# Reordering filler matmuls and gate projections in a graph recurrence

## The chip, the core and the metric

The kernel runs on one core of a Trainium2 chip. The metric is device time in microseconds (us) of one execution; the table below gives three timed runs and one profiled execution. The core's engines work side by side, each on its own instructions in their written order: TensorE (PE in the profile; PEld are its weight loads), VectorE (DVE), ScalarE (ACT), GpSimd (POOL) and SyncE (SP, which only issues DMAs here). They wait for each other through semaphores. "Matmul" below means one call of the program on float32 data with 256 columns; the trace shows each as two passes of the array ("x24" is 12 calls), and two passes start 0.22 us apart at full clock, so that one call is 0.447 us.

## The reference, cut to what matters

Sixteen graphs of 1024 nodes with 256 features go through four residual layers. Layers 0, 1 and 3 are dense products with the adjacency matrix and are not touched. Layer 2 is a recurrence over the nodes:

```python
norm_adjT = jnp.swapaxes(adj, 1, 2) * dinv[:, :, None]
def step(h, i):
    x = jnp.take(h_e, i, axis=1)
    row = jnp.take(norm_adjT, i, axis=1)
    x_par = jnp.einsum('bj,bjd->bd', row, h)
    iou = x @ W_ioux.T + b_ioux + x_par @ W_iouh.T + b_iouh
    r, z = jnp.split(iou, 2, axis=1)
    r, z = (jax.nn.sigmoid(r), jax.nn.sigmoid(z))
    hc = jnp.tanh(x @ W_coux.T + b_coux + x_par * r @ W_couh.T + b_couh)
    h_new = z * x_par + (1.0 - z) * hc
    return jax.lax.dynamic_update_slice(h, h_new[:, None, :], (0, i, 0)), None
h_out, _ = jax.lax.scan(step, h_e, jnp.arange(n))
```

Node i sees the new values of nodes before it and the old values of those after it.

## The kernel before, in words

Layer 2 handles the nodes in 8 blocks of 128 (t = 0 to 7), each in 8 sub-blocks of 16 (s = 0 to 7). In the 128 nodes of a block an earlier step of the kernel has put mutually independent nodes next to each other, so that the 16 nodes x 16 graphs of a sub-block can mostly be computed at once. A sub-block consists of

- `x`, the weighted sum over the parents (L967 on VectorE): a base part held in `bxt` (SBUF) plus `near`, the contribution of the sub-block just finished, made by four matmuls (L1037; at the end of a block `next_block`, L771);
- a round (`round_`): matmuls into `pr` and `pz`, sigmoids (L843, L848), r times x (L844), matmuls into `pc`, tanh, the new values `hT`; then `turned`, which transposes them into `h` (L870, L873);
- a run-time branch (L1014) for a further round, `one_more`, where chains of dependent nodes ask for it;
- the scatter of `h` to HBM into `hs_d` (L1030, two indirect DMAs issued by GpSimd).

What does not depend on the chain serves as filler for TensorE: the lists `share`, `behind` and the gates' tasks.

`Gates` (L734) makes the input half of the three gates of the *next* sub-block: GpSimd copies the nodes' features into `hs` (L740), and `gate(q)` does four matmuls (L749) into one PSUM buffer `pf` (there are three of them, shared by all filler) and gives back `out`, the copy with bias to SBUF. q = 0 is r, q = 1 is z, q = 2 the candidate. For z and the candidate `out` is one VectorE instruction (L754), for r it is two ScalarE instructions (L757). Afterwards `seed_r` and `seed_zc` (L761, L764, L765) put them into the PSUM accumulators. Outs are collected in `late` and issued at the next `evict()`.

For s = 0 the gates of sub-block 1 are made inside the round, as part of `todo`. For s = 1 to 7 they are made in the arms of the branch: within `one_more`, or, where it isn't needed, in the Else arm, all three one after the other with their outs one behind. Instructions after the branch that read something which `one_more` may rewrite, such as `h`, wait for a count of the writing engine's semaphore. In the built program the Else arm makes up for `one_more`'s instructions by a larger step (21) on the first instruction of an engine in that arm, and the last one brings the count to the arm's end. `near` (L1037) waits for ScalarE's count at the arm's end (974 in one of the places), for VectorE's 3351, which the first VectorE out of the arm passes, and for TensorE's own last gate matmul; L771 and the scatter L1030 wait for ScalarE's alone.

`base_tasks(t + 1)` (L597) makes `bxt` of the next block: for each of the 16 graphs a task of seven matmuls (L637), one for each block of 128 parents except block t, from adjacency `ab` and features `hb`. The features come from three places: `hn_d` for blocks long finished, `hs_d[t - 1]` for the block finished last (L609), and `he_d` for those still old. So the matmul over parent block t - 1, the one with index k = t - 1 of the seven, needs the DMA L609, which reads what the scatter at the end of block t - 1 has written. A mask (L615, GpSimd) is laid over one tile of `ab`. `last_tasks` (L666) adds the last missing part of `bxt` from `hr`, 512 KB loads out of `hs_d` (L675). SyncE issues in this order after a block's last scatter: three `hr` loads, L609 for graph 0, L609 for graph 1, a copy to `hn_d` (L943).

For s = 0, `todo` is the three gates (cost 1.72 each), the seven base matmuls of graph 0 (0.43 each, `share`) and up to 16 `last_tasks` (0.4 each, `behind`). `fill(weight)` takes tasks from its front: a first portion before `x` is computed, a second one (weight 1.3) inside the round after the `pc` matmuls, the rest in `turned`. `todo` is a fixed list, and for the four compute engines layer 2 keeps the written order; only SyncE's order is chosen by the framework's scheduler.

Where layer 2 ends, the first additions of layer 3 (L1113, VectorE) stand early in block 7 and need `hs_d[6]` too.

Of the kernel before, what the change touches and what calls it, by code (L numbers as in the profile page):

```python
# [40 lines left out]
def gnn_stack(ctx: ExitStack, tc: tile.TileContext, a: dict, out: bass.AP):  # L41
# [520 lines left out]
    def layer_2(shared, early):  # L562
        with ExitStack() as st:
# [102 lines left out]
            def last_tasks(t, bxt):  # L666

                n = P - S
                loaded = {}

                def load(b0):
                    ao = big.tile([P, 4, n], F32, name="ao", bufs=3)
                    nc.sync.dma_start(ao, next_d[b0 : b0 + 4, t - 1].rearrange("b p i -> p b i"))
                    hr = big.tile([P, 4, D], F32, name="hr", bufs=3)
                    nc.sync.dma_start(hr, hs_d[t - 1][b0 // GB][b0 % GB * P : (b0 % GB + 4) * P]  # L675
                                      .rearrange("(b p) d -> p b d", p=P))
                    loaded[b0] = ao, hr

                def task(b):
                    def run():  # L680
                        b0 = b - b % 4
                        ao, hr = loaded[b0]
                        if b % 4 == 0 and b + 12 < B:
                            load(b + 12)
                        pl = psum.tile([P, DC, n], F32, name="pf", bufs=3)
                        for c in range(DC):
                            nc.tensor.matmul(pl[:, c], hr[:, b - b0, c * P : (c + 1) * P], ao[:, b - b0],
                                             start=True, stop=True)
                        to = bxt[:, :, b, S:]
                        return lambda: nc.vector.tensor_add(to, to, pl)  # L690
                    return 0.4, run
                for b0 in (0, 4, 8):
                    load(b0)
                return [task(b) for b in range(B)]

            def load_he(t):
                he = big.tile([P, DC, B, P], F32, name="he")
                for c in range(DC):
                    nc.sync.dma_start(he[:, c], heT_d[:, :, c, t * P : (t + 1) * P].rearrange("b p i -> p b i"))
                return he  # L700
# [4 lines left out]
            class Sub:  # L705
# [3 lines left out]
                def __init__(self, t, s):  # L709
                    self.s = s  # L710
                    self.n = P - s * S + (S if t + 1 < NT else 0)
                    self.aj = big.tile([P, G2, P + S], F32, name="aj")
                    for g in range(G2):
                        nc.gpsimd.indirect_dma_start(out=self.aj[:, g], out_offset=None, in_=near_d[:, :],
                                                     in_offset=row(0, g, t, s))
# [18 lines left out]
            class Gates:  # L734


                def __init__(self, he, s):
                    self.hs = big.tile([P, DC, G2 * GR], F32, name="hs")
                    for c in range(DC):
                        nc.gpsimd.tensor_copy(self.hs[:, c].rearrange("p (b i) -> p b i", b=B),  # L740
                                              he[:, c, :, s * S : (s + 1) * S])
                    self.g = big.tile([P, 3, DC, G2 * GR], F32, name="gates")
                    self.tasks = [lambda q=q: self.gate(q) for q in (1, 2, 0)]

                def gate(self, q):
                    pg = psum.tile([P, DC, G2 * GR], F32, name="pf", bufs=3)
# [28 lines left out]
            def far_tasks(bxt, h, sub):  # L775


                bd, s = sub.bd, sub.s
                far = P - (s + 2) * S

                def task(g, c, b4):
                    def run():
                        pf = psum.tile([P, 4, far], F32, name="pf", bufs=3)
                        nc.tensor.matmul(pf, h[:, g, c * P : (c + 1) * P], bd[:, g, b4 : b4 + 4, S : S + far],  # L784
                                         start=True, stop=True)
                        to = bxt[:, c, g * GB + b4 : g * GB + b4 + 4, P - far :]
                        return lambda: nc.vector.tensor_add(to, to, pf)  # L787
                    return 0.0067 * far, run
                tasks = []
                if far > 0:  # L790
                    tasks = [task(g, c, b4) for g in range(G2) for c in range(DC) for b4 in (0, 4)]
                if sub.n > P - s * S:
                    tasks.append((0.9, lambda: next_block(h, bd, P - (s + 1) * S, s == 0)))
                return tasks
# [103 lines left out]
            with tc.manual_schedule(engines={mybir.EngineType.PE, mybir.EngineType.DVE, mybir.EngineType.Activation, mybir.EngineType.Pool}):  # L898
# [17 lines left out]
                behind = []  # L916
                for t in range(NT):
# [10 lines left out]
                    for s in range(NS):  # L928
# [4 lines left out]
                        share = [task for _ in range(BASES[s] if base_todo else 0) for task in base_todo.popleft()]  # L933
                        todo, gx_next = [], None
                        if s == 0:
                            gx_next = Gates(he, 1)
                            todo = [(1.72, task) for task in gx_next.tasks] + share + behind
                        else:
                            if s == 1 and t + 1 < NT:
                                he_next = load_he(t + 1)  # L940
                            if s == 1 and t > 0:
                                for g in range(G2):
                                    nc.sync.dma_start(hn_d[g * GB : (g + 1) * GB, (t - 1) * P : t * P],  # L943
                                                      hs_d[t - 1][g].rearrange("(b p) d -> b p d", p=P))
                            lists = [behind, share]
                            sizes = [len(x) for x in lists]
                            while any(lists):
                                i = max(range(2), key=lambda i: len(lists[i]) / max(sizes[i], 1))
                                todo.append(lists[i].pop(0))
# [83 lines left out]
                        if s + 1 < NS:  # L1033
# [5 lines left out]
                            behind = far_tasks(bxt, h, sub)  # L1039
                        elif t + 1 < NT:  # L1040
                            next_block(h, sub.bd, 0, False)
                            near = pnx
                            behind = last_tasks(t + 1, bxt_next)
# [172 lines left out]
    with tc.tile_pool(name="shared", bufs=2) as shared:  # L1216
        x, hn, at = {}, {}, {}
        layer_2(shared, lambda: early_3(shared, x, hn, at))
        layer_3(shared, x, hn, at)
# [46 lines left out]
```

## Time and profile before

| what | us |
|---|---|
| three timed runs | 4899.82, 4900.79, 4907.13 (median 4900.79) |
| profiled execution | 4910.16 |
| its span, first to last instruction | 4908.1 |
| layer 2, from 1507 to 3450 in the span | 1943.0, TensorE busy 1748.29 of it |
| mean granted TensorE clock | 0.975 |

How to read the profile's lines. In the timeline a line gives start, duration, engine, source line, operation, what is written<-read, shape and number of instructions merged, and in brackets the idle time of that engine before it with what ended the idle time. SPq is SyncE issuing DMAs. In the list of waits a line gives who waited for whom, the total in us, how often and the longest. The windows view gives, for a stretch of time, each engine's busy time, the granted TensorE clock (1.00 is full), the DMA engines' share and GB/s.

### The profile page before, as it was taken

What the parts mean: (1) busy time and instruction counts of PE and PEld (TensorE: products, weight loads), DVE (VectorE), ACT (ScalarE), POOL (GpSimd) and SP (SyncE); (2) the same over time, 40 slices, a digit from 0 to 9 for tenths busy, and PEclk for the clock granted to TensorE, in tenths of its full rate; (3) what the DMA queues carried; (4) which work ended last, traced back from release to release, by engine and by line L of the source; (5) the groups of instructions that cost most, each with busy time, mean ns of one, the idle gap of its engine ahead of it and who ended that gap; (6) DMA issues with size and microseconds to landing.
All of it is one profiled execution on the core that took longest, in us unless ns stands there. A gap on an engine that the chain in (4) does not pass through costs nothing. (4 is left out here: it accounts for less than half of the span.)

```text
span 4908.1 us, 52731 instructions
## 1 busy us (share of the span) xinstructions
PE 4510.6 (92%) x18307; PEld 3022.5 (62%) x18307; DVE 2290.3 (47%) x6408; ACT 1213.9 (25%) x2651; POOL 1586.5 (32%) x1947
## 2 busy tenths in 40 slices
PE   8898899999987999899999999988799999999999
PEld 4443455555555777777777777777465555555656
DVE  6667754465553444444444444344524334344342
ACT  1211112122211222222322222222223223223232
POOL 3122233443333322232222323232524334234231
PEclk9999999999998999999999999999899999999999
DMA  5333326545536444444444444430422222232200
GB/s 159 116 91 102 93 81 205 182 165 182 173 121 186 126 150 126 151 126 148 125 139 123 142 145 141 124 110 32 167 69 86 77 93 71 77 103 72 74 26 17
DMA packets 530980, 576.65 MB, mean 117 GB/s; under 512 B 42544, under 2 KB 439472, under 8 KB 528304
## 3 DMA queue, kind: packets, MB, share of 16 engines
q1 hardware_dynamic: 499536, 460.27, 30.3%
q0 software_dynamic: 31040, 111.44, 6.4%
q8 instruction: 199, 3.26, 0.3%
q14 instruction: 205, 1.68, 0.1%
HBM read 469.65 MB, written 116.65 MB: 119 GB/s over the span
## 5 line engine op out<-in xcount | busy, mean ns | idle before, releaser
L309 PE MATMUL pa<-at,h 128*128 128x512 f32 x1088 | 493.8, 606 | 32.8 <-DVE ag L314 32.8
L1141 PE MATMUL ph<-ag,w 128*128 128x512 f32 x1024 | 478.3, 610 | 32.6 <-DVE hh L1145 32.6
L637 PE MATMUL pf<-hb,ab 128*128 128x256 f32 x1568 | 435.1, 390 | 22.1 <-ACT bs L624 18.8
L1179 PE MATMUL po<-w,hh 128*128 128x256 f32 x2048 | 447.7, 379 | 0.0
L1179 PEld LDWEIGHTS po<-w,hh 128*128 128x128 f32 x2048 | 387.8, 190 | 59.3 <-issue 7.9
L309 PE MATMUL pa<-at,q 128*128 128x512 f32 x960 | 424.3, 595 | 0.0
L749 PE MATMUL pf<-hs,wx 128*128 128x256 f32 x1536 | 358.3, 390 | 30.0 <-POOL hs L740 30.0
L309 PEld LDWEIGHTS pa<-at,h 128*128 128x128 f32 x1088 | 209.0, 195 | 276.5 <-issue 230.7
L1141 PEld LDWEIGHTS ph<-ag,w 128*128 128x128 f32 x1024 | 178.5, 190 | 294.3 <-DVE hh L1145 151.7
L749 PEld LDWEIGHTS pf<-hs,wx 128*128 128x128 f32 x1536 | 297.5, 196 | 74.8 <-POOL hs L740 33.1
L1147 POOL TENSOR_TENSOR ss<-ss,sq 128x512 f32<-128x512 f32 x224 | 305.3, 1363 | 117.8 <-ACT sq L1144 113.4
L637 PEld LDWEIGHTS pf<-hb,ab 128*128 128x128 f32 x1568 | 280.8, 195 | 69.8 <-ACT bs L624 26.1
L309 PEld LDWEIGHTS pa<-at,q 128*128 128x128 f32 x960 | 178.2, 190 | 215.8 <-issue 212.8
L1030 POOL DMA_INDIRECT hs_d<-h,table x128 | 129.4, 1011 | 490.6 <-ACT gates L757 386.9
L1145 DVE TENSOR_SCALAR hh<-ph,b 128x512 f32<-128x512 f32 x256 | 190.1, 747 | 153.6 <-ACT sq L1144 120.1
L784 PE MATMUL pf<-bd,h 128*128 128x384 f32 (+5 forms) x768 | 221.9, 376 | 26.8 <-DVE bxt L787 26.8
L1126 PE MATMUL pa<-bxt,h 128*128 128x512 f32 x512 | 228.7, 599 | 18.6 <-POOL bxt L1108 18.6
L1126 PE MATMUL pa<-at,h 128*128 128x512 f32 x512 | 228.8, 597 | 0.0
L1144 ACT ACTIVATE sq<-ph,b 128x512 f32<-128x512 f32 x224 | 153.8, 687 | 233.1 <-PE ph L1141 187.9
L1171 ACT ACTIVATE hh<-hh,rw 128x512 f32<-128x512 f32 x256 | 168.9, 714 | 138.4 <-DVE hh L1170 136.6
L754 DVE TENSOR_TENSOR gates<-pf,bias 128x512 f32<-128x512 f32 x128 | 88.4, 691 | 231.6 <-PE pf L749 231.6
L1182 DVE TENSOR_TENSOR x<-x,po 128x256 f32<-128x256 f32 x120 | 50.5, 421 | 288.9 <-PE po L1179 288.9
(253 smaller groups left out, 7411.4 us busy)
## 6 DMA issues: line engine op xcount, KB each, us to landing
at<-in_adjT SPq DMA_DIRECT2D x64, 1024.0 KB
ab<-in_adj SPq DMA_DIRECT2D x128, 512.0 KB
bxt<-in_adjT SPq DMA_DIRECT2D x64, 512.0 KB
at<-in_adjT SPq DMA_DIRECT2D x64, 512.0 KB
ad<-in_adj SPq DMA_DIRECT2D x128, 128.0 KB
x_d<-x POOLq DMA_DIRECT2D x16, 1024.0 KB, 4.8
he_d<-h POOLq DMA_DIRECT2D x16, 1024.0 KB, 9.1
heT_d<-hT POOLq DMA_DIRECT2D x16, 1024.0 KB
```

The source lines that it names most:

```text
L309: nc.tensor.matmul(pa, h[:, mt, c * P : (c + 1) * P], at[n0 // 512][:, mt], start=mt == 0, stop=mt == NT - 1)
L637: nc.tensor.matmul(pb, ab[:, jts[k]], hb[:, jts[k]], start=k == 0, stop=k == len(jts) - 1)
L749: nc.tensor.matmul(pg[:, e], wx[:, c, q * D + e * P : q * D + (e + 1) * P], self.hs[:, c], start=c == 0, stop=c == DC - 1)
L784: nc.tensor.matmul(pf, h[:, g, c * P : (c + 1) * P], bd[:, g, b4 : b4 + 4, S : S + far], start=True, stop=True)
L1030: nc.gpsimd.indirect_dma_start(out=hs_d[t][g][:, :], out_offset=row(1, g, t, s), in_=h[:, g], in_offset=None)
L1126: nc.tensor.matmul(pa, h[b][:, mt, c * P : (c + 1) * P], at[b][n0 // NH][:, mt], start=mt == 0, stop=mt == NT - 1)
L1141: nc.tensor.matmul(ph, w1[:, c, k * P : (k + 1) * P], ag[:, c, n0 : n0 + NH], start=c == 0, stop=c == DC - 1)
L1144: nc.scalar.activation(sq, ph, AF.Square, bias=b1[:, k : k + 1])
L1145: nc.vector.tensor_scalar(hh[:, k], ph, b1[:, k : k + 1], None, op0=ALU.add)
L1147: nc.gpsimd.tensor_tensor(ss, ss, sq, ALU.add)
L1171: nc.scalar.activation(hh[:, k], hh[:, k], AF.Silu, scale=rw[:, k : k + 1])
L1179: nc.tensor.matmul(po, hh[:, c, k * P : (k + 1) * P], w2[:, c], start=c == 0, stop=c == HC - 1)
```

## The change

It has two parts. The gates' tasks are made in the order r, z, candidate instead of z, candidate, r, everywhere. And at s = 0 the first six of the seven base matmuls of graph 0 stand ahead of the gates in `todo`; the seventh stays behind them.

```diff
-                    self.tasks = [lambda q=q: self.gate(q) for q in (1, 2, 0)]
+                    self.tasks = [lambda q=q: self.gate(q) for q in range(3)]
...
                         if s == 0:
                             gx_next = Gates(he, 1)
-                            todo = [(1.72, task) for task in gx_next.tasks] + share + behind
+                            todo = share[:6] + [(1.72, task) for task in gx_next.tasks] + share[6:] + behind
```

In the built program this gives at the start of blocks 1 to 6 on TensorE, from `near` (L771) to the round's `pr` matmuls: before, 12 gate matmuls; after, 6 base matmuls and the 8 gate matmuls of r and z. Behind the `pc` matmuls there follow, before, 7 base matmuls; after, the 4 of the candidate and 1 base matmul; then `last_tasks` as before. The base matmul with k = t - 1 carries the wait for L609 in both. In block 0, where `behind` is empty, 8 gate matmuls stood ahead of the round, 4 gate and 4 base matmuls behind `pc`, 3 base matmuls behind the transposes; now 6 base matmuls stand ahead, the 8 of r and z behind `pc`, the candidate's 4 and the seventh base matmul behind the transposes, and the first base matmul waits for two loads and the mask. In block 7 there is no base work: `share` is empty. On GpSimd the two masks at s = 0 come ahead of the two `aj` DMA issues (L714) instead of behind them. In the Else arms ScalarE's two L757 instructions follow the first gate instead of the last, and VectorE's two L754 follow the second and third. SyncE's order is the same.

## The prediction

> **What bounds the kernel now.** I read the page first, then the list of waits on TensorE, then the timeline around a block's start, then the windows view for the clock.
>
> ```profile
> span 4908.1 us, 52731 instructions
> PE 4510.6 (92%) x18307; PEld 3022.5 (62%) x18307; DVE 2290.3 (47%) x6408; ACT 1213.9 (25%) x2651; POOL 1586.5 (32%) x1947
> ```
>
> TensorE is the bound, but in layer 2 it is idle for 1943.0 - 1748.29 = 195 us, and all it does there hangs on one chain. What counts is which wait ends last at a place, so here are three of its waits:
>
> ```profile
> PE pa L1037 <- ACT gates L757: 41.6, 42, 1.0
> ...
> PE pf L749 <- POOL hs L740: 30.0, 10, 10.9
> ...
> PE pnx L771 <- ACT gates L757: 5.2, 7, 0.9
> ```
>
> 42 times `near` waits 0.99 us for ScalarE's copy of gate r, the last thing in the Else arm; seven more times at a block's end (0.62 to 0.91). The start of block 2:
>
> ```profile
> 1996.38 0.69 DVE L754 TENSOR_TENSOR gates<-pf,bias 128x512 f32<-128x512 f32 x1 [1.40 <-PE pf L749]
> ...
> 1999.83 0.84 ACT L757 ACTIVATE gates<-pf,bias 128x256 f32<-128x256 f32 x2 [5.18 <-PE pf L749]
> ...
> 2000.35 1.16 PE L771 MATMUL pnx<-bd,h 128*128 128x128 f32 x8 [0.62 <-ACT gates L757]
> ...
> 2000.94 1.04 POOL L1030 DMA_INDIRECT hs_d<-h,table  x1 [15.12 <-ACT gates L757]
> ...
> 2003.43 1.73 SPq L675 DMA_DIRECT2D hr<-hs_d  x3
> ...
> 2003.74 7.13 PE L749 MATMUL pf<-hs,wx 128*128 128x256 f32 x24 [2.23 <-POOL hs L740]
> ...
> 2005.21 0.98 SPq L609 DMA_DIRECT2D hb<-hs_d  x2
> ...
> 2010.71 1.89 PE L802 MATMUL pr<-x,wh 128*128 128x256 f32 x8
> ...
> 2015.89 3.19 PE L637 MATMUL pf<-hb,ab 128*128 128x256 f32 x14
> ```
>
> The scatter starts when ScalarE's copies end; GpSimd copies `hs` after both scatters, so TensorE stands 2.23 us; the base matmuls come 15.5 us after `near`. L609 lies behind 1.5 MB of `hr`; by the trace's DMA completions it lands at 2011.70, 10.8 us after the scatter started (blocks 1 to 6: 11.7, 10.8, 11.0, 11.5, 10.7, 11.6). Today it is 4 us early. Block 7 shows the same chain as a wait, 11.2 us:
>
> ```profile
> 3243.02 1.04 POOL L1030 DMA_INDIRECT hs_d<-h,table  x1 [15.41 <-ACT gates L757]
> ...
> 3254.20 0.96 DVE L1113 TENSOR_TENSOR hb<-hb 128x768 f32<-128x768 f32 x1 [9.23 <-DMA hb<-hs_d]
> ```
>
> The clock is decided in stretches of 3.41 us (columns: stretch, length, PE, PEld, DVE, ACT, POOL busy, clock, DMA share, GB/s):
>
> ```profile
> 2001.42:2004.84 3.42, 1.19 (x6) 0.99 (x6) 1.36 (x3) 0.60 (x1) 2.95 (x5) 1.00 0.33 80
> 2004.84:2008.25 3.41, 3.41 (x10) 2.70 (x9) 0.69 (x1) 0.00 (x0) 1.87 (x4) 0.50 0.92 305
> 2008.25:2011.66 3.41, 3.41 (x17) 3.00 (x17) 0.69 (x1) 0.75 (x2) 0.00 (x0) 1.00 1.24 427
> ...
> 3380.41:3383.82 3.41, 3.32 (x14) 3.20 (x15) 0.91 (x4) 0.28 (x1) 1.00 (x3) 0.50 0.02 5
> 3383.82:3387.23 3.41, 3.41 (x18) 3.41 (x17) 1.24 (x5) 1.03 (x4) 0.00 (x0) 0.50 0.00 0
> ```
>
> A stretch with 2.2 us idle is followed by one at half clock (1.7 us lost); a half-clock stretch that is itself not quite full (0.09 idle) is followed by another.
>
> **The change, part by part.**
>
> *Gate r first, sub-blocks 1 to 6.* The matmuls are the same. ScalarE's copies follow the first gate, two gates (3.5 us: 1996.38 against 1999.83) earlier, so `near` no longer waits for them. Does the wait pass to VectorE, whose last copy (0.69, like ScalarE's 0.84 begun 0.1 after the last gate) is now last? If so the gain is 0.15 each, 6 us in all; if nothing is left it is 41.6. `near` needs VectorE's count only up to the arm's first copy, which ends while the last gate runs, and TensorE's own last matmul, for which I leave 0.1: **-37** (42 x 0.89). The candidate's copy, 0.69, lies beside `near` (1.16), before `x` needs VectorE; `seed_r` comes earlier on ScalarE. Where `one_more` runs, r's copies stand before the sigmoids but end within the `pr` matmuls: nothing. The earlier scatters have no reader before the block's end.
>
> *Start of blocks 1 to 6.* `near` gains its 0.62 to 0.91 and the wait for `hs` goes: with the scatter 3.45 us earlier `hs` is there in time even without the moved matmuls. But the base matmul k = t - 1, second of six in block 2, now comes 1.5 us after `near` starts, where the wait for L609 has no cover. Landing, block 2: 2011.70 - 3.45 = 2008.25, if the path runs as fast. It won't quite: the scatter then shares the DMA engines with graph 1's base load, which runs until about 2000. Scatters alone land 2.3 to 2.4 after their start, scatters beside such a load 5.5 to 6.6 (2787.69, 3028.61), each some 2.4 after the load's end; by that rule the blocks lose 0, 2.3, 1.5, 2.0, 1.4, 1.4 (bounds 0 and 4). So it lands at 2010.5; TensorE does one base matmul, stands from 2001.2 to 2010.6, then 5 base (2.2) and 8 gate matmuls (3.6), plus the clock. The stall covers whole stretches, so work resumes within a half-clock stretch, and by the rows above the next is half too: 1.7 to 3.4 lost, taken 2.56. `pr` then starts at 2019.0 instead of 2010.71: +8.3. The same sum gives +7.4, +8.3, +7.0, +7.9, +7.5, +6.4: **+44.6**. Given back: two matmuls fewer behind `pc`, 12 x 0.447 = **-5.4**; that stretch is TensorE's own (14 passes of L637, then L687 without a gap). Added: the second `last_tasks` call needs the buffer of the candidate, whose copy stands behind VectorE's `hT` work, about 0.35 each: **+2.1** (0 to 4).
>
> The Trainium skill, "TensorE: Matmul & The Clock Gate", Part 1, states a free-running window of 3413 ns, half clock after at least one idle window, full clock again after one busy window; its section on oscillation warns of just this, a DMA wait longer than a window that starts every tile cold. The rows differ twice: 2.2 us idle suffice, and a nearly full half-clock window doesn't restore the clock. By the page's rule each stall would cost 1.7 at most and the forecast would be an estimated 5 us lower. The measurement decides.
>
> *Block 0.* TensorE is free at 1521.3; gates started at 1522.55, `pr` at 1526.10. Now the first base matmul needs graph 0's features, landed at 1524.64, and the mask, which GpSimd has ready at about 1523.3. From 1524.75 six matmuls (2.7) run at half clock, since the stretch to 1523.56 is mostly idle: `pr` at 1530.1, +4.0; behind the transposes five matmuls instead of three, +0.8: **+4.8**. The `aj` issues, 3.7 us later behind the masks, are needed only when `h` is done: nothing.
>
> *Block 7* has no base work: L1113 lands 3.7 us earlier and holds VectorE less, which delayed `pc` by 3.76; one L754 fewer stands ahead of r's product: **-4.0** (-3 to -5).
>
> *Other moves.* Masks (0.55) before `aj` at blocks 1 to 6 find their load landed: nothing. The sub-blocks shift against the clock's stretches; 16 stretches in layer 2 lie at or over 1.7 us idle, some by such phase: 0, bounds -5 and +5.
>
> Sum: -37 + 44.6 - 5.4 + 2.1 + 4.8 - 4.0 = **+5 us**. Against the profiled execution that is 4910.16 to 4915; the median of the runs is 9.4 below it, and I carry the difference over: 4901 + 5 = **4906**. No change that a measurement can tell means within 0.2%, 9.8 us.
>
> **The rivals.**
>
> *A. The stall is longer, slower.* Place: L609's landing at blocks 1 to 6. Each further microsecond costs 6 us; from 0.8 us a block on it is slower by over 0.2%. For it: the scatter beside a load (up to 4 us more), `hr` loads beside it, two full half-clock stretches. At +2 us a block: 4918.
>
> *B. The stall is shorter, faster.* The graph-1 load ends before the scatter's packets flow, and the clock loses one stretch: -8.6 and -5, with the phases' -5: 4887 at the far end, 4892 in the middle. Against it: the DMA flow of 329 GB/s seen between 1998 and 1999.
>
> *C. The wait passes to VectorE.* `near` still stands 0.85 us, 42 times: +31, 4937. For it: VectorE's copy is the arm's last instruction. Against it: the count it waits for.
>
> *D. The second part does what it seems for*, fills the wait for `hs` with no stall: -37 - 4 - 6 x 2.9 - 5, 4838. That needs L609's data 9 us earlier; nothing speaks for it.
>
> **How the numbers follow.** My forecast 0.42 (within 0.2%), A 0.30, C 0.08, B 0.16, D 0.04. Faster 0.20, same 0.42, slower 0.38. The forecast's own range is 4892 to 4910; for 8 in 10 it reaches through B's far end and A at 3.5 us a block, leaving out D and most of C: 4886 to 4927.
>
> **What would show it.** In the profile after: the wait of L1037 for ScalarE's gates gone and no other over 0.2 in its place (C: one for VectorE's L754); base matmuls at s = 0 of blocks 1 to 6 waiting for hb<-hs_d, 7 to 10 us each, in the sum over 45 us; the scatter starting before the last gate ends; the wait for `hs` gone; two half-clock stretches after each stall; in block 7 `pc` waiting under 3.8. I am wrong if the stalls are under 5 us or over 11, or if TensorE's part behind `pc` is not its own and the delay is caught up there.

## The result, and the profile after

The changed kernel took 4907.8 us (median of 4 runs, 4903.9 to 4911.7), the kernel before 4904.0 beside it: a ratio of 1.0008, interval 0.9991 to 1.0026. Forecast was 4906, no difference that can be told. The profiled execution took 4911.68 us, of which 4909.6 are the span; before it was 4910.16 and 4908.1. So little moved at the end, and much moved inside. The page's head:

```profile
span 4909.6 us, 52727 instructions
PE 4521.0 (92%) x18307; PEld 3029.4 (62%) x18307; DVE 2288.1 (47%) x6408; ACT 1218.7 (25%) x2651; POOL 1584.7 (32%) x1947
```

TensorE does the same 18307 matmuls and is busy 10.4 us longer: a first sign that its clock was granted less (0.970 in the mean, before 0.975). What TensorE waits for (total us, times, longest):

```profile
PE pf L637 <- DMA hb<-hs_d: 44.6, 6, 9.1
...
PE pf L749 <- POOL hs L740: 16.0, 3, 12.8
...
PE pf L687 <- DMA hr<-hs_d: 7.0, 7, 1.9
...
PE pa L1037 <- DVEq L1016: 5.6, 6, 0.9
PE pa L1037 <- DVEq L1014: 5.5, 8, 0.7
...
PE pf L637 <- DMA hb<-he_d: 4.6, 1, 4.6
```

The 41.6 us in which `near` (L1037) stood for ScalarE's gates and the 5.2 us of L771 are gone. Each of the 42 joins keeps a gap of 0.10 us, too short for this list, and VectorE took none of them over. The six waits after `one_more` stay nearly as long but are now put down to VectorE (L1016: 5.6; before 5.9, put down to ScalarE), and so is one more wait of under a microsecond (L1014: 5.5 in 8; before 4.6 in 7). The waits for `hs` fell from 30.0 to 16.0: those at the starts of blocks 1 to 6 and the one of 1.2 in block 0 are gone, and block 7's is 0.73 instead of 2.23. In their place six base matmuls (L637) wait 44.6 us for rows of `hs_d`, once in each of blocks 1 to 6. The start of block 2, which the prediction used, shows how (timeline; start, busy, engine, line):

```profile
2000.68 2.54 PE L749 MATMUL pf<-hs,wx 128*128 128x256 f32 x11
...
2000.98 1.04 POOL L1030 DMA_INDIRECT hs_d<-h,table  x1 [11.67 <-ACT gates L757]
...
2003.06 1.05 PE L771 MATMUL pnx<-bd,h 128*128 128x128 f32 x8
...
2003.95 0.60 PE L637 MATMUL pf<-hb,ab 128*128 128x256 f32 x2
...
2005.87 1.46 SPq L675 DMA_DIRECT2D hr<-hs_d  x3
2007.37 1.07 SPq L609 DMA_DIRECT2D hb<-hs_d  x2
...
2013.63 4.37 PE L637 MATMUL pf<-hb,ab 128*128 128x256 f32 x10 [9.09 <-DMA hb<-hs_d]
...
2017.84 3.62 PE L749 MATMUL pf<-hs,wx 128*128 128x256 f32 x16
...
2021.29 1.03 PE L802 MATMUL pr<-x,wh 128*128 128x256 f32 x4
```

The scatter now starts while the gates still run, and `near` starts without a wait. 1.5 us after it has begun, TensorE has come to the one base matmul that needs the block just scattered (the second), and its load lies behind three loads of `hr`. By the trace's DMA completions L609 lands at 2013.59, 12.6 us after the scatter's start. The same stretch by the clock's own stretches (columns: stretch, length, PE, PEld, DVE, ACT, POOL busy, clock, DMA share, GB/s):

```profile
2003.94:2007.36 3.42, 0.60 (x4) 0.20 (x2) 1.36 (x4) 0.60 (x1) 2.55 (x5) 1.00 0.37 78
2007.36:2010.77 3.41, 0.00 (x0) 0.00 (x0) 0.00 (x0) 0.00 (x0) 0.00 (x0) 0.50 0.90 308
2010.77:2014.18 3.41, 0.55 (x1) 0.50 (x2) 0.00 (x0) 0.00 (x0) 0.00 (x0) 0.50 1.15 396
2014.18:2017.60 3.42, 3.42 (x9) 2.70 (x8) 0.00 (x0) 0.00 (x0) 0.00 (x0) 0.50 0.35 153
2017.60:2021.01 3.41, 3.41 (x17) 3.00 (x16) 0.00 (x0) 0.84 (x2) 0.00 (x0) 1.00 0.00 0
```

PE, DVE, ACT and POOL all stand while the DMA engines move 300 to 400 GB/s, and when TensorE resumes it does nine matmuls in a stretch where the next one holds 17. Block 7, which has no base work, profits: its load lands 9.6 us after the start of `near` instead of 11.8, and `pc` waits for VectorE's r product 2.04 instead of 3.76 us. First the line of before, then those after:

```profile
3256.75 3.05 PE L802 MATMUL pc<-r,wh 128*128 128x256 f32 x8 [3.76 <-DVE r L844]
```

```profile
3256.28 1.04 POOL L1030 DMA_INDIRECT hs_d<-h,table  x1 [11.95 <-ACT gates L757]
...
3267.72 0.96 DVE L1113 TENSOR_TENSOR hb<-hb 128x768 f32<-128x768 f32 x1 [5.81 <-DMA hb<-hs_d]
...
3269.66 2.77 PE L802 MATMUL pc<-r,wh 128*128 128x256 f32 x7 [2.04 <-DVE r L844]
```

### The profile page after: what moved, and what is told of

It reads as the page before. It is cut to its first block, busy times and chain, and to the rows that moved or that the text cites. A ratio compares the mean times of both kernels' runs of the same rounds, so it can differ in the third digit from the quotient of the medians.

```text
span 4909.6 us, 52727 instructions
## 1 busy us (share of the span) xinstructions
PE 4521.0 (92%) x18307; PEld 3029.4 (62%) x18307; DVE 2288.1 (47%) x6408; ACT 1218.7 (25%) x2651; POOL 1584.7 (32%) x1947
## 5 line engine op out<-in xcount | busy, mean ns | idle before, releaser
L637 PE MATMUL pf<-hb,ab 128*128 128x256 f32 x1568 | 451.9, 401 | 72.2 <-DMA hb<-hs_d 44.6
L637 PEld LDWEIGHTS pf<-hb,ab 128*128 128x128 f32 x1568 | 289.1, 201 | 126.1 <-DMA hb<-hs_d 46.8
L754 DVE TENSOR_TENSOR gates<-pf,bias 128x512 f32<-128x512 f32 x128 | 88.4, 690 | 373.7 <-PE pf L749 363.8
```

The costliest lines, as they stand in the source:

```text
L637: nc.tensor.matmul(pb, ab[:, jts[k]], hb[:, jts[k]], start=k == 0, stop=k == len(jts) - 1)
```

## The experiments

The theory is that the change is two changes that pull against each other: an order that gains at 42 joins and at seven block starts, and base matmuls that give it back through one matmul in seven. All ratios are to the kernel before, run on the same chip beside the experiment.

### The order alone

```diff
-                    self.tasks = [lambda q=q: self.gate(q) for q in (1, 2, 0)]
+                    self.tasks = [lambda q=q: self.gate(q) for q in range(3)]
```

> The order r, z, candidate alone; the gates stay ahead of all base matmuls, as before. My theory is that the two parts of the change pull against each other: the order gains, the six base matmuls lose. Gain of the order: 42 joins of near (L1037) that no longer stand for ScalarE's gates, -37; at the starts of blocks 1 to 7 the waits for hs (2.2 us) and of L771 (0.7 us) go, about -20; the half-clock stretch that follows those 2.2 us goes with them, 1.7 us a block, -8; block 7 -4. Together about -67: 4837 us, 4825 to 4850, ratio to before 0.986. No matmul of L637 stands for hs_d at a block's start. Rival 1, the order itself gives little (its joins turn into another wait, or the earlier scatter is worth nothing) and the base matmuls cost little: 4885 to 4905, and the small net result of the change would be small parts, not two large ones. Rival 2, the gates wait for hs just as before, because GpSimd's copies and not the scatter are late: hs waits 2.2 us seven times still, 4860.

Measured: 4838.9 us, ratio 0.9862 (0.9847 to 0.9877), **67.8 us faster** than the 4906.7 of before. The start of block 2 in its timeline:

```profile
1986.08 1.04 POOL L1030 DMA_INDIRECT hs_d<-h,table  x1 [11.66 <-ACT gates L757]
...
1988.16 1.05 PE L771 MATMUL pnx<-bd,h 128*128 128x128 f32 x8
...
1989.05 5.35 PE L749 MATMUL pf<-hs,wx 128*128 128x256 f32 x24
...
1994.23 1.89 PE L802 MATMUL pr<-x,wh 128*128 128x256 f32 x8
```

The gates follow `near` without a gap, since the scatter is out early enough for GpSimd to have `hs` copied. `pr` starts 6.1 us after the start of `near`; before it was 10.4, with the change 18.2. (In the other blocks it is 6.1 to 6.4, but 10.2 in block 4, where TensorE stands within `near` and before the gates, and the profile names no engine for it.) Both rivals fall: the net of the change is two large parts, and the wait for `hs` was the scatter's. This version is faster than the kernel before and than the changed one.

### The base matmuls alone

```diff
-                            todo = [(1.72, task) for task in gx_next.tasks] + share + behind
+                            todo = share[:6] + [(1.72, task) for task in gx_next.tasks] + share[6:] + behind
```

> The six base matmuls alone; the gates stay in the order z, candidate, r. My theory: the stall at the starts of blocks 1 to 6 is there and is longer than the 6.0 to 9.1 us seen with the change, because the scatter starts at the last gate's end again, some 3 us later; L609 lands 11.3 to 12.3 us after near starts, as in the profile of before, so each stall is 8.5 to 11 us, in the sum 55 to 62, and pr starts 8 to 9 us later than before in each of six blocks. The wait of L1037 for ScalarE's gates (41.6 us) stays. About +50 with the half clock and the 12 matmuls fewer behind pc: 4953 us, 4940 to 4970, ratio 1.010. Rival, the base matmuls are nearly free and the order gave little: under 4920, with stalls under 5 us each.

Measured: 4954.2 us, ratio 1.0104 (1.0089 to 1.0120), some 47 us slower. TensorE's waits:

```profile
PE pf L637 <- DMA hb<-hs_d: 48.6, 6, 9.9
PE pa L1037 <- ACT gates L757: 41.6, 42, 1.0
...
PE pf L637 <- DVE x L967: 4.3, 5, 0.9
```

The stalls were 6.7 to 9.9 us, in the sum 48.6, under the 55 to 62 that I expected: the landing was 10.8 to 12.1 after `near`, about half a microsecond earlier than foreseen, and part of the time (4.3) was another wait just ahead of the stall, for VectorE's `x`. `pr` still came 50.3 us later in the six blocks together, within the 8 to 9 a block expected, and so did the time.

The parts don't add up: -67.8 and +47.4 would make -20; together they measured +3.8. Both take away the same 2.2 us wait for `hs` at the block starts (the order by an earlier scatter, the base matmuls by standing in front of it), so one of the two gains nothing there. That can explain only the part that lies between `near` and `pr`: 9.5 of the 28 us by which the profiles' blocks 1 to 6 miss the sum. The other 18 lie between `pr` and the next `near`, nearly all of it time at half clock: 3.4 us less than before with the order, 6.8 less with the base matmuls, 6.4 more with both. Why is not shown.

### The parent's block last among the base matmuls

```diff
-                jts = [j for j in range(NT) if j != t - 1]
+                jts = [j for j in range(NT) if j not in (t - 1, t - 2)] + ([t - 2] if t > 1 else [])
```

> The whole change, with one thing moved: in each list of seven base matmuls the parent block t - 2, whose rows come through hs_d (L609), is the last, so that the six ahead of the gates need only data landed long before. The sum has the same terms in another order. My theory is that the one matmul that reads hs_d makes the whole loss of the second part: the 44.6 us of L637 waiting for hb<-hs_d fall under 8, the half-clock stretches after them go, the gain of the order stays: 4837 us, 4825 to 4855, ratio 0.986, within 0.3% of the order alone. Rival 1, six matmuls ahead of the gates cost time for themselves (pr comes 2.7 us later at every block's start): 16 us over the order alone, 4853. Rival 2, another wait of the same length stands behind the stall (GpSimd's copies, the masks, the buffers of pf): 4880 or more.

Measured: 4845.4 us, ratio 0.9882 (0.9866 to 0.9897). No wait for `hb<-hs_d` is left among TensorE's waits; the one of block 0 is:

```profile
PE pf L749 <- POOL hs L740: 15.2, 3, 10.5
...
PE pf L687 <- DMA hr<-hs_d: 6.1, 6, 1.5
...
PE pf L637 <- DMA hb<-he_d: 3.5, 1, 3.5
```

Six matmuls still stand ahead of the gates; only which six has changed, and 62 us came back. That settles where the loss sits: in one matmul's operand, neither in the number ahead nor in a wait hidden behind the stall. It is 6.5 us over the order alone, and the two intervals overlap; the profile shows 4.9 us in block 0 (242.2 from the layer's first gate to the next block's `near`, against 237.3). So the moved matmuls, even with their data there in time, gain nothing over the order alone.

### `hr` loaded behind L609

```diff
-                    if t == NT - 1:
-                        early()
...
                         base_todo = base_tasks(t + 1, bxt_next)
+                    if t > 0:
+                        behind = last_tasks(t, bxt)
+                    if t == NT - 1:
+                        early()
...
-                            behind = last_tasks(t + 1, bxt_next)
+                            behind = []
```

> The whole change, with SyncE's loads of ao and hr (L673, L675) issued at the next block's start, behind the two of L609, instead of ahead of them. Three hr loads of 512 KB now land at 9.9, 11.8 and 13.2 and L609's 128 KB at 13.6 in block 2 of the profile with the change, one after another, 1.4 to 1.9 each. My theory is that the place in SyncE's queue sets the stall: L609 lands 4 to 5 us earlier, the stalls of L637 on hb<-hs_d fall from 44.6 to between 12 and 22 in the sum, hr may be waited for up to 2 us a block: 4880 us, 4868 to 4895, ratio 0.995. Rival 1, the scatter and its landing set it, the place in the queue nothing: stalls still 40 or more, 4905. Rival 2, hr, now last, becomes the wait behind the gates: stalls short but 4 to 5 us of hr<-hs_d in each block, 4905 again.

Measured: 4859.0 us, ratio 0.9909 (0.9894 to 0.9925), better than my 4880 and outside the 4868 to 4895 that I gave. TensorE's waits:

```profile
PE pf L637 <- DMA hb<-hs_d: 8.8, 5, 3.4
PE pf L687 <- DMA hr<-hs_d: 5.5, 5, 1.8
```

And the start of block 2, in its timeline (L1032 is the scatter here):

```profile
1988.13 1.04 POOL L1032 DMA_INDIRECT hs_d<-h,table  x1 [11.66 <-ACT gates L757]
...
1992.87 0.33 SPq L609 DMA_DIRECT2D hb<-hs_d  x1
...
1993.24 1.58 SPq L675 DMA_DIRECT2D hr<-hs_d  x3
1994.87 0.57 SPq L609 DMA_DIRECT2D hb<-hs_d  x1
...
1995.10 4.07 PE L637 MATMUL pf<-hb,ab 128*128 128x256 f32 x10 [3.40 <-DMA hb<-hs_d]
```

Only graph 0's load moved ahead of `hr`, and it is the one that matters. It lands 6.9 us after the scatter's start (1995.05), against 12.6: the place in SyncE's queue makes 5.7 us of the path, the scatter and its landing the rest. I had counted 4 to 5. The stalls shrank to 0.4 to 3.4 us, and of the six blocks only block 2, with the longest, kept a half-clock stretch ahead of `pr`, which takes off more than the waits alone. `hr`, now last, is waited for less than with the change (5.5 against 7.0). Both rivals fall.

### The order at the joins alone

```diff
-                    self.tasks = [lambda q=q: self.gate(q) for q in (1, 2, 0)]
+                    self.tasks = [lambda q=q: self.gate(q) for q in (range(3) if s else (1, 2, 0))]
```

> The kernel before with the order r, z, candidate for the gates of sub-blocks 1 to 7 alone; those of sub-block 0, computed at the end of the block before, keep z, candidate, r; no base matmul is moved. It divides the 67.8 us that the order alone saved. My theory: the 42 joins carry 37 of it (0.89 each), the starts of blocks 1 to 7 with their hs and L771 waits and their half-clock stretch the other 31: 4869 us, 4858 to 4880, ratio 0.9925; the wait of L1037 for ScalarE's gates gone, the one of L771 (5.2) and the hs waits of 2.2 still there. Rival 1, the joins carry nearly all: 4845. Rival 2, the joins carry little, since the wait passes on, and the starts carry it: 4890 or more.

Measured: 4864.6 us, ratio 0.9915 (0.9902 to 0.9929), **41.6 us** faster. TensorE's waits keep those of the block starts:

```profile
PE pf L749 <- POOL hs L740: 33.0, 10, 11.5
...
PE pnx L771 <- ACT gates L757: 5.2, 7, 0.9
```

The joins carry 41.6 (35 to 48) of the order's 67.8; the other 26, by subtraction, belong to the seven block starts and whatever the clock does behind them.

### Three base matmuls ahead

```diff
-                            todo = share[:6] + [(1.72, task) for task in gx_next.tasks] + share[6:] + behind
+                            todo = share[:3] + [(1.72, task) for task in gx_next.tasks] + share[3:] + behind
```

> The whole change, with three base matmuls ahead of the gates in place of six. The parent block's matmul is number k = t - 1, so it is among the three in blocks 1, 2 and 3 and behind the gates in blocks 4, 5 and 6. My theory, that only this one matmul's wait counts: blocks 1 to 3 stand for hb<-hs_d 7.9 to 9.1 us each and last 10, 15 and 12 us longer than with the order alone, as with the change; blocks 4 to 6 have no such wait and last as with the order alone; block 0 stands 4 to 5 for hb<-he_d. 4839 + 37 + 6 = 4882 us, 4872 to 4892, ratio 0.995; hb<-hs_d 25 us in 3 waits. Rival, each base matmul ahead costs its own share: hb<-hs_d as before or in six shorter waits, and blocks 4 to 6 longer by 4 to 6 us each.

Measured: 4873.8 us, ratio 0.9935 (0.9922 to 0.9948).

```profile
PE pf L637 <- DMA hb<-hs_d: 25.4, 3, 9.2
...
PE pf L637 <- DMA hb<-he_d: 4.1, 1, 4.1
```

Three waits, in blocks 1 to 3, and none in 4 to 6. From the start of `near` to the start of the next block's, blocks 1 to 3 took 246.8, 244.8 and 266.2 us (order alone 239.8, 231.1, 252.6), blocks 4 to 6 249.1, 232.3 and 228.5 (252.8, 231.9, 228.3). The cost goes with the parent's matmul, block by block.

### The order z, r, candidate

```diff
-                    self.tasks = [lambda q=q: self.gate(q) for q in (1, 2, 0)]
+                    self.tasks = [lambda q=q: self.gate(q) for q in (1, 0, 2)]
```

> The kernel before with the order z, r, candidate; no base matmul is moved. In both orders with the candidate last the last copy is VectorE's, and r, the one that ScalarE copies, has a gate's matmuls behind it. My theory, that the engine of the last copy makes the gain and not the place of r for its reader: the wait of L1037 for ScalarE's gates gone all the same, the scatter at about -0.6 us from near at a block's end in place of -2.3, so that hs is waited for up to 1 us seven times: 4846 us, 4836 to 4857, ratio 0.9875. Rival, r must be first (its copy in the second place is still what near or the scatter stands for): L1037's wait for ScalarE's gates stays at over 15 us in the sum, 4865 or more.

Measured: 4851.3 us, ratio 0.9892 (0.9878 to 0.9907). The wait of L1037 for ScalarE's gates is gone here too, so what matters at a join is that ScalarE's gate isn't the last. At the block starts the scatter begins 0.1 to 0.9 us ahead of `near` instead of 1.8 to 2.1, and the gates stand 1.1 to 1.7 us each (TensorE's waits; those that the profile puts down to "issue" follow the same copy):

```profile
PE pf L749 <- POOL hs L740: 22.3, 6, 13.0
...
PE pf L749 <- issue: 5.5, 4, 1.7
```

That is longer than the 1 us expected; the rival's 15 us at the joins didn't come.

## Why the prediction was right

The time and the reason held: two large terms of opposite sign, each in the place that the prediction named. That the total came out within 2 us is in part luck, as two of its parts missed by about 8 us each, in opposite directions. By its steps, with `near` taken from its start:

*Joins, -37.* Right. The trace after has a gap of 0.10 us, put down to no engine, at each of the 42 joins where before it had 0.99: that is the 0.89 of the sum, 37.4 in all. The experiment with the joins alone measured -41.6 (35 to 48), which agrees. Rival C, the wait passing to VectorE, did not come: a gap of 0.10 leaves no room for VectorE's last copy.

*Start of blocks 1 to 6, +44.6.* Right in mechanism, too dear by about 8.5. `pr` starts 15.6 to 18.2 us after `near`, where before it was 8.7 to 10.4: +40.7 over six blocks, less the 4.6 that the `near` at their ends no longer waits, is +36.1. Two parts of the term were too big. L609 landed 11.0 to 12.6 us after the scatter's start, 11.8 in the mean, where the prediction's landings make 12.65: 5 us in six blocks. The slower scatter was sized nearly right: SyncE issued the first `hr` load 7.6 us later after the scatter in the six blocks together, where I had 8.6. The other 4 us are the loads themselves: from that issue to L609's landing they took 7.7 to 8.5 us, before 8.2 to 9.2, and I had left that as it was; why they ran faster is not shown. And the clock cost 1.5 to 2.4 us a block, 1.95 in the mean (half of TensorE's busy time within half-clock stretches between `near` and `pr`), not 2.56. Two or three stretches at half clock did follow each stall's begin, but in the first of them TensorE stood for part or all of the time, where it costs nothing. The stalls, 6.0 to 9.1 and 44.6 in the sum, came out just under the 7 to 10 and "over 45" that I had named as the sign.

*The rest of blocks 1 to 6.* Here the forecast gained too much by 7.5, and this hid the error above. 30 of the 42 joins lie in these six stretches from `pr` to the next `near`: 30 x 0.89, 5.4 given back and 2.1 added make -30; with the 4.6 of `near` set apart likewise, measured is -22.5. (The 5.4 is 0.2 too much: in a run of gate matmuls the passes start 0.216 us apart, so a call is 0.432 and not 0.447.) The half clock there cost 21.8 us against 15.4 before (+6.4, beyond the 5 that I had given the phases), the waits at L687 grew from 5.0 to 7.8 in these stretches, those for `hr` from 3.4 to 6.2 (block 2's, 1.94 us, alone is longer than half a clock stretch), and those of L802 by 1.0. Whether the change causes the rest of the half clock or only meets the grid badly stays open: the same sum was 8.5 to 13.7 in six of the experiments and 5.1 in the one with the order z, r, candidate, with the same recurring gaps. From `near` to `near` the six blocks together took 13.6 us longer; the prediction's terms make 14.6, by two errors that cancel.

*Block 0, +4.8.* The stretch from the layer's first gate to block 1's `near` took 244.4 (244.6 before), about what six joins gained and the base matmuls cost by the prediction (-0.5). Against the order alone the six ahead cost 7.1 here, with the 4.6 us wait for `he_d`.

*Block 7, -4.0.* From its `near` to the last scatter 208.7 became 197.8, -10.9; the joins' 6 x 0.89 and the 4.0 make -9.3. The `hs` wait of its own start, 2.23 to 0.73, which I had booked only for blocks 1 to 6, is as large as the difference.

*The rule of the Trainium skill.* "TensorE: Matmul & The Clock Gate", Part 1, would have made the clock cost 1.7 us at most per stall. The measured mean of 1.95 lies nearer to that than to my 2.56. In the rows the page is right that a fully busy stretch restores the clock (2014.18 to 2017.60, then 1.00); the half-clock stretch before it was 0.55 busy and restored nothing. My row with 0.09 us idle, which was to show that a nearly full half-clock stretch restores nothing either, is an exception. In the nine profiles, between 1507 and 3230 us, all 51 half-clock stretches with under 0.45 us idle were followed by full clock and all 35 with over 0.5 by another half. So what a stall cost depended on where in its stretch the work resumed: 1.5 us in block 1, where the stretch had 0.39 idle, and 2.0 in block 2, where it had 2.86.

The remainder, +2.3 us ahead of layer 2 and -3.2 behind it, is where no instruction changed. Rival D, a second part with no stall, would need other operands: with the parent's block last it is what one gets, 4845 where D had 4838.

## What to carry to other kernels

Moving work forward to fill a wait can pay only if each of its operands has landed by then: go through the operands one by one, and follow the latest one's load back through its queue to the write it reads. Here it gained nothing even then, since the other part had already removed the wait. At a join after a branch, find out up to which instruction of the branch each engine is waited for: here the join stood for ScalarE's copy when that came last, and not for VectorE's when that did, so the engine that the next work needs least should end the branch. When a change with two parts measures nothing, run the parts apart before dropping both: here one was worth 1.4% and the other cost it, and reordering seven matmuls or three loads recovered most.

## What the runs showed that was not expected

Through most of layer 2 the half clock has a sharp edge. Cut along the clock's own stretches of 3.41 us, the rows of the nine profiles (layer 2 from 1507 to 3230 us) show 116 full-clock stretches in which TensorE idled 1.71 us or more: 107 were followed by a half-clock stretch. Of 220 with 1.0 to 1.70 us none was. So there the edge lies at half a stretch, and gaps of about 1.1 us that lie beside other small ones cost 1.7 us or nothing, depending on where the grid cuts them. It isn't a rule for all work: from 3230 to 3450 us, mostly block 7, 17 of 75 stretches with 1.0 to 1.70 us idle were followed by half clock, and what makes the difference is not shown. With the order z, r, candidate, single waits of 1.1 to 1.7 us at the block starts cost no clock at all, and the profiled execution lost only 5.1 us to the clock behind `pr`, where the changed kernel's lost 21.8.
